# What lies behind, added by sixteen 32 by 32 products instead of four of 32 by 128; the bias of the exponentials as an operand

## The chip, the cores and the metric

The kernel runs on one core of a Trainium2 chip. The metric is the time of an execution on the device in microseconds. An engine of the core is named as in the profile: PE is TensorE (PEld its weight loads), DVE is VectorE, ACT is ScalarE, POOL is GpSimd, SP is SyncE, which issues most DMAs. A name with a q at its end is that engine's sequencer.

## What is computed

The input x has 4096 rows of 64 numbers, adj is a 4096 by 4096 matrix of zeros and ones (64 MB of float32). Each row of x is normalized, clipped at zero and multiplied by a weight matrix; every row of the output is x plus a weighted sum of these rows. The neighbours of a row (the non-zero columns of adj) are ranked from the left, and only the last 100 count: the rightmost one has weight 1, and the weight halves with each step to the left.

```python
h = jnp.maximum(_layernorm(x, axis=-1), 0.0)
support = h @ weight
mask = (adj != 0).astype(support.dtype)
rank = jnp.cumsum(mask, axis=1)
deg = rank[:, -1:]
k = jnp.minimum(deg, 100.0)
pos = rank - (deg - k)
w = mask * jnp.where(pos > 0, 0.5 ** (k - pos), 0.0)
out = x + w @ support + bias
```

## The kernel before

The weight of a neighbour depends on how many neighbours stand to its right. The kernel finds this number with matrix products, writes it so that one byte holds the exponent, and lets an exponential on ACT turn the byte into the weight.

Rows are worked on in groups of 512 (W), and for each group the right half of the columns first, then the left half: 16 units (u) of 512 rows by 2048 columns. A unit has four loads of 1 MB, `load` (L120), issued by SP into eight buffers a_sb; so there are 64 loads in all. SP issues a load when the buffer's last reader, eight loads earlier, is done. For each load:

- `convert` (L341 on DVE, three times L339 on ACT) turns 128 rows of float32 into bytes m.
- `transpose` (L352, PE) turns them, four bytes at a time as one float32, into pt in PSUM; `settle` (L363, L361, DVE) copies this to mt in SBUF. Columns of adj now lie on partitions.

For each unit:

- `totals` (L369, PE) counts the neighbours in stretches of 32 columns: eight products of 128 by 32 weights, two sets of four, the second set added to the first. `split` (L379, ACT) and `divide` (L382, DVE) take the counts apart, `carry` (L388, POOL) brings in what the right half counted.
- `suffix` (L396, PE) adds up what stands to the right of each stretch; `clamp` (L400, DVE) limits it and writes `behind`, [128, 512] in float16.
- `place(u, a)`, twice a unit, a = 0 and 1 (L407 and L412, PE), makes four tiles v, each 128 by 512 float32, one bank of PSUM. Tile j takes what lies behind from the 32 partitions 32j to 32j+31 of `behind`, through the matrix `where` (L407, a product with 32 rows and 128 columns of weights, which begins the sum in the bank), and then, 32 by 32, the count inside each stretch from `tri` (L412, sixteen products, four on each tile, which end it). There are five buffers for v, so a place needs the release of three of the four tiles of the place before it; the last wait is on the fourth product of L407.
- `weigh` (L420, ACT), once for each v, reads two of the four bytes of every word of v, 1024 bytes on each partition, and writes the exponential to wk. Its scale is -ln 2 and its bias -38 ln 2. There are 128 weigh instructions: 122 on whole tiles, and 6 on half tiles for the last three tiles of all. Three of the last tiles are done on DVE and POOL instead (`encode` L426, `take` L431, `lower` L439, then `gather`).
- `aggregate` (L453, PE) multiplies wk with the support rows hr (two parts, high and low) into acc.

For each group of 512 rows `drain` (L469, ACT, with the bias of the layer as a [128,1] operand bias_sb; the very last half L467 on DVE), `turn_back` (L476, PE) and `finish` (L483, L484, DVE) add the sum to x; `store` (L491) and L486 write it out.

What runs when is set by a list of tasks with costs in nanoseconds and due times, from which the order on each engine is planned while the program is built; a table of shifts (L497 to L523) changes the due times by hand. After that each engine runs its instructions strictly in this order. Neither the costs nor the shifts are touched by the change. L193 makes a [128,1] tile `floor` that holds -38 ln 2; the kernel before does not read it.

Of the kernel before, what the change touches and what calls it, by code (L numbers as in the profile page):

```python
# [8 lines left out]
F32 = mybir.dt.float32  # L9
# [6 lines left out]
U8 = mybir.dt.uint8  # L16
AF = mybir.ActivationFunctionType
# [8 lines left out]
SUB = 32  # L26
UNIT = 2.0 ** -9
LN2 = 0.6931471805599453
# [3 lines left out]
def kernel(  # L32
# [34 lines left out]
    nc = tc.nc  # L67
    P = 128
# [9 lines left out]
    W = TG * P  # L78
# [24 lines left out]
    ps_v = ctx.enter_context(tc.tile_pool(name="ps_v", bufs=NV, space=bass.MemoryType.PSUM))  # L103
# [68 lines left out]
    for h in range(H):  # L172
        q = slice(h * D, (h + 1) * D)
# [18 lines left out]
    floor = const.tile([P, 1], F32, name="floor")  # L192
# [3 lines left out]
    where = const.tile([P, 2, P], F16, name="where")  # L196
# [131 lines left out]
    low, codes, masks, words, wts, accs, tots, pts, sums8, behind, vs, signed = {}, {}, {}, {}, {}, {}, {}, {}, {}, {}, {}, (1, 7, 15)  # L328
# [73 lines left out]
    def place(u, a):  # L402

        for j in range(4):
            v = vs[u, 4 * a + j] = ps_v.tile([P, W], F32, tag="v", name="v")
            q = slice(SUB * j, SUB * (j + 1))
            nc.tensor.matmul(v, where[q, a, :], behind[u][q, :], start=True, stop=False, skip_group_check=True)  # L407
        for c in range(4):
            for j in range(4):
                q = slice(SUB * j, SUB * (j + 1))  # L410
                m = masks[u][q, c, :, a] if UNITS[u][2] == CB else masks[u][q, c % 2, :, c // 2]
                nc.tensor.matmul(vs[u, 4 * a + j][SUB * c:SUB * (c + 1), :], tri[q, q], m, start=False, stop=True,  # L412
                                 skip_group_check=True)

    def weigh(u, k, part=None):
        r = slice(0, W) if part is None else slice(part * W // 2, (part + 1) * W // 2)
        if not part:
            wts[u, k] = wpool.tile([P, 2, W], F32R, name="wk")
        v = vs[u, k] if part == 0 else vs.pop((u, k))
        nc.scalar.activation(wts[u, k][:, :, r], v.bitcast(U8).rearrange("p (i f) -> p f i", f=4)[:, :2, r], AF.Exp, scale=-LN2, bias=-38.0 * LN2)  # L420

    def encode(u, k):

# [150 lines left out]
    for u, (g, c0, cb) in enumerate(UNITS):  # L574
# [9 lines left out]
        for k in range(2 * cb):  # L584
            due = at + k
            if k % 4 == 0:
                task(place, (u, k // 4), PE, due, 800, 920, [("clamp", u), ("constants", 1)], ("v", *(("encode" if (u, k + j) in QUICK else "weigh", u, k + j, *((1,) if u == U - 1 and k + j in PARTED else ())) for j in range(4))))
            if u == U - 1 and k in PARTED:
                continue
            weighs = "weigh"  # L590
            piece_of = block(u, k) // (HB // 2)
            if (u, k) in QUICK:
                weighs = "take"
                task(encode, (u, k), DVE, due - 8, 1160, 1300, [("place", u, k // 4), ("convert", NT - 2)])
                task(take, (u, k), DVE, due - 8, 690, 820, [("encode", u, k)], ("w", ("gather", u, k)))
                task(lower, (u, k), POOL, due - 8, 1200, 1300, [("second", piece_of // 2, piece_of % 2), ("convert", NT - 3)])
            else:
                task(weigh, (u, k), ACT, due + 2.5, 1000, 1130, [("place", u, k // 4)], ("w", ("aggregate", u, k)))
            task(gather if (u, k) in QUICK else aggregate, (u, k), PE, due + 14, 480, 720, [(weighs, u, k), ("lower", u, k) if (u, k) in QUICK else None, ("second", piece_of // 2, piece_of % 2)] +
                 ([("drain", g - 1)] if g and head and k == 0 else []))  # L600
        for part in range(2 if u == U - 1 else 0):
            for k in PARTED:
                due = at + k + part
                task(weigh, (u, k, part), ACT, due + 2.5, 570, 700, [("place", u, k // 4)], None if part else ("w", ("aggregate", u, k, 1)))
                task(aggregate, (u, k, part), PE, due + 14, 260, 500, [("weigh", u, k, part)])
# [20 lines left out]
    while kinds:  # L626
        heads = []
        for kind, keys in kinds.items():
            f, args, engine, rank, hold, lag, needs, pool = tasks[keys[0]]
# [10 lines left out]
        f, args, _, _, hold, lag, _, pool = tasks[key]  # L640
# [11 lines left out]
    for at, _, f, args in sorted(order, key=lambda o: o[:2]):  # L652
        if f in (turn, spread, support, count, transpose, totals, suffix, place, aggregate):
            if end is not None and at - end > 700:
                warm(int(at - end) // 215)
            end = None if f is spread or end is None else at + tasks[f.__name__, *args][4]
        f(*args)
# [37 lines left out]
```

## Time and profile before

| | |
|---|---|
| median of 3 runs | 190.86 us (190.5 to 191.04) |
| the profiled execution | 190.5 us, of which the span of the profile is 188.8 us |
| granted PE clock | mean 0.979 of full speed |
| PE busy | 171.8 us (91%), 1499 products |
| PE weight loads busy | 107.7 us (57%) |
| DVE busy | 161.7 us (86%) |
| ACT busy | 149.5 us (79%); L420 120.0 us of it, x128, mean 1015 ns |
| POOL busy | 20.4 us (11%) |
| HBM | 367 GB/s over the span |
| L407 | 128 products of 32 by 128, mean 383 ns |
| L412 | 512 products of 32 by 32, mean 394 ns |

The span is what the profiler saw of the program; 1.7 us of the execution's time lie around it. Busy times of PE overlap: products are pipelined, and the time of one is longer than the distance to the next. A row of the timeline shows when a run of like instructions began, how long it was from its first start to its last end, which engine and line, what it wrote and read, and how many there were; brackets hold the idle time before it and what ended it. A row of a source line shows the shortest, median and longest time of one instruction in nanoseconds, then the first and last start.

### The profile page before, as it was taken

The numbers are of one execution on the slowest core, as the hardware profiler recorded it, in microseconds if no ns is written. First come the engines' busy times: TensorE is split into PE (matmuls) and PEld (weight loads), VectorE is DVE, ScalarE is ACT, GpSimd is POOL, SyncE is SP. The second block draws the span as 40 slices with busy tenths as digits, with TensorE's granted clock in tenths as the row PEclk, the third lists the DMA queues.
The fourth block names the chain that finished last, engine by engine and source line by source line (L and its number), as shares of the span: only waits on it lengthen the run. The fifth ranks groups of instructions, "written<-read, shape, count | busy, mean of one in ns | idle before, by whom it ended". The sixth has DMA issues, their size and how long they took to land.

```text
span 188.8 us, 3797 instructions
## 1 busy us (share of the span) xinstructions
PE 171.8 (91%) x1499; PEld 107.7 (57%) x1499; DVE 161.7 (86%) x221; ACT 149.5 (79%) x176; POOL 20.4 (11%) x60
## 2 busy tenths in 40 slices
PE   7879979898989999999979997999799999999980
PEld 5657746655555565466546554655366545554560
DVE  4834758899999999999999989998999899996743
ACT  2298055789899896999897889787978997899970
POOL 7000035020001000100020002000100029001000
PEclk9999687999999999999999999999999999999998
DMA  6999999999999999999999999999999999931000
GB/s 212 417 422 422 415 427 420 417 415 420 420 422 420 420 417 418 429 422 413 422 420 420 422 417 418 420 425 418 420 422 410 424 420 418 418 128 62 21 3 28
DMA packets 10338, 69.49 MB, mean 368 GB/s; under 512 B 1360, under 2 KB 1616, under 8 KB 2128
## 3 DMA queue, kind: packets, MB, share of 16 engines
q1 hardware_dynamic: 10016, 69.15, 88.6%
q8 instruction: 12, 0.20, 0.4%
q10 hardware_dynamic: 304, 0.10, 0.2%
q14 instruction: 6, 0.05, 0.1%
HBM read 68.19 MB, written 1.05 MB: 367 GB/s over the span
## 4 chain that ended last, share of the span: by engine, by line
PE 49%; DVE 29%; DMA 10%; ACT 5%; POOL 3%; issue 2%; POOLq 0%; ACTq 0%; DVEq 0%
PE acc L453 18%; DVE m L341 13%; DMA a_sb<-in_adj_dram 10%; PE pt L352 10%; DVE mt L363 6%; PE v L412 4%; PE v L407 4%; ACT wk L420 3%; PE pc L265 2%; PE tot L369 2%; PE pd L281 2%; PE ps L396 2%; DVE behind L400 2%; PE po L476 2%; ACT mt L260 1%
## 5 line engine op out<-in xcount | busy, mean ns | idle before, releaser
L420 ACT ACTIVATE wk<-v 128x1024 fp32r<-128x1024 uint8 (+1 forms) x128 | 120.0, 1015 | 15.3 <-PE v L412 14.9
L341 DVE TENSOR_SCALAR m<-a_sb 128x2048 uint8<-128x2048 f32 x61 | 84.9, 1394 | 4.2 <-DMA a_sb<-in_adj_dram 4.1
L453 PE MATMUL acc<-wk,hr 128*128 128x512 f32 (+1 forms) x256 | 77.7, 421 | 1.1 <-ACT acc_sb L469 0.6
L453 PEld LDWEIGHTS acc<-wk,hr 128*128 128x128 f32 x256 | 43.4, 189 | 18.6 <-issue 6.3
L352 PE MATMUL pt<-ident,m 128*128 128x128 f32 x256 | 41.2, 286 | 6.0 <-DVE m L341 5.4
L363 DVE COPY mt<-pt 128x512 uint32<-128x512 uint32 x61 | 41.7, 685 | 4.3 <-PE pt L352 4.3
L352 PEld LDWEIGHTS pt<-ident,m 128*128 128x128 f32 x256 | 29.7, 145 | 20.6 <-PE acc L453 4.8
L388 POOL COPY sums<-behind 1x512 f16<-1x512 f16 x8 | 6.8, 852 | 129.6 <-ACT sums L379 109.5
L407 PE MATMUL v<-behind,where 32*128 32x512 f16 x128 | 13.7, 383 | 1.5 <-DVE behind L400 1.1
L412 PE MATMUL v<-mt,tri 32*32 32x512 f16 x512 | 14.2, 394 | 0.0
L379 ACT ACTIVATE sums<-tot 128x512 f16<-128x512 uint8 x16 | 9.7, 608 | 3.5 <-PE tot L369 3.5
L400 DVE TENSOR_SCALAR behind<-ps,excess 128x512 f16<-128x512 f32 x16 | 11.9, 745 | 0.1
L382 DVE CAST sums<-tot 128x512 f16<-128x512 uint8 x16 | 10.9, 683 | 1.1 <-ACT sums L379 1.1
L369 PE MATMUL tot<-mt,band 128*32 128x512 f16 x128 | 10.2, 393 | 0.3 <-DVE mt L363 0.3
L396 PE MATMUL ps<-sums,later 128*128 128x512 f16 x32 | 10.0, 396 | 0.2 <-DVE sums L382 0.2
L407 PEld LDWEIGHTS <-where 32*128 32x128 f16 x128 | 3.7, 90 | 10.3 <-issue 9.8
L412 PEld LDWEIGHTS <-tri 32*32 32x32 f16 x512 | 4.4, 88 | 8.7 <-issue 8.7
L248 PE MATMUL none<-junk 128*128 128x256 bf16 x44 | 7.9, 362 | 1.1 <-DVE junk L133 1.1
L260 ACT ACTIVATE mt<-px 64x512 f32<-64x512 f32 x8 | 4.2, 585 | 4.9 <-PE px L256 4.8
L339 ACT ACTIVATE m<-a_sb 128x2048 int8<-128x2048 f32 x3 | 7.6, 2547 | 0.0
L248 PEld LDWEIGHTS <-junk 128*128 128x128 bf16 x44 | 5.6, 129 | 3.4 <-DVE junk L133 1.1
L272 ACT ACTIVATE xs<-pc 128x512 f32<-128x512 f32 x4 | 2.3, 610 | 6.0 <-PE pc L265 6.0
(87 smaller groups left out, 100.6 us busy)
## 6 DMA issues: line engine op xcount, KB each, us to landing
a_sb<-in_adj_dram SPq DMA_DIRECT2D x64, 1024.0 KB, 16.5
xr<-in_x_dram SPq DMA_DIRECT2D x2, 512.0 KB, 6.3
out_dram<-xr SPq DMA_DIRECT2D x1, 512.0 KB, 18.4
out_dram<-xr SPq DMA_DIRECT2D x1, 384.0 KB, 2.3
out_dram<-xr ACTq DMA_DIRECT2D x1, 64.0 KB, 1.6
out_dram<-xr SPq DMA_DIRECT2D x1, 64.0 KB, 1.7
w<-in_L_gnn_weight_dram ACTq DMA_DIRECT2D x2, 16.0 KB, 6.0
bias_sb<-in_L_gnn_bias_dram SPq DMA_DIRECT2D x1, 0.2 KB, 14.1
```

Source lines behind the costliest of these rows:

```text
L248: nc.tensor.matmul(none[:, :2 * P], junk[:, :P], junk, start=True, stop=True)
L341: nc.vector.tensor_scalar(m_v, a_v, 0.0, 64.0, op0=ALU.not_equal, op1=ALU.add)
L352: nc.tensor.transpose(pts[n][:, c, :], m32[:, c * P:(c + 1) * P], ident)
L363: nc.vector.tensor_copy(mw, pt)
L369: nc.tensor.matmul(tot[SUB * c:SUB * (c + 1), :], band[:, SUB - 12 - 4 * a:2 * SUB - 12 - 4 * a], masks[u][:, c, :, a], start=(a == 0), st ...
L382: nc.vector.tensor_copy(*bytes_of(u, 1))
L396: nc.tensor.matmul(px, later[cb][:r, f, :], sums[:r, f, :], start=(f == 0), stop=(f == 1))
L400: nc.vector.tensor_scalar(behind[u], pts.pop((u, "s")), excess[UNITS[u][2]], float(MAX_NEIGH), op0=ALU.subtract, op1=ALU.min)
L407: nc.tensor.matmul(v, where[q, a, :], behind[u][q, :], start=True, stop=False, skip_group_check=True)
L412: nc.tensor.matmul(vs[u, 4 * a + j][SUB * c:SUB * (c + 1), :], tri[q, q], m, start=False, stop=True, skip_group_check=True)
L420: nc.scalar.activation(wts[u, k][:, :, r], v.bitcast(U8).rearrange("p (i f) -> p f i", f=4)[:, :2, r], AF.Exp, scale=-LN2, bias=-38.0 * LN2)
L453: nc.tensor.matmul(accs[g][:, r], parts.rearrange("p s d -> p (s d)"), wk[:, s, r], start=(k == s == 0 and c0 + cb * E * P == N), stop=(c0 ...
```

## The change

Two things change. In `place` the four products of L407, each with 32 rows by 128 columns of weights, become sixteen products of 32 by 32, one for each tile j and each quarter c of its partitions; they all come before the products of L412, which are left as they were. In `weigh` the bias is no longer a constant in the instruction: it is read from the tile `floor`, one number on each partition. In the changed kernel the two lines of place are L409 and L414, that of weigh L422, and every later line moves by two.

```diff
@@ def place(u, a) @@
         for j in range(4):
-            v = vs[u, 4 * a + j] = ps_v.tile([P, W], F32, tag="v", name="v")
-            q = slice(SUB * j, SUB * (j + 1))
-            nc.tensor.matmul(v, where[q, a, :], behind[u][q, :], start=True, stop=False, skip_group_check=True)
+            vs[u, 4 * a + j] = ps_v.tile([P, W], F32, tag="v", name="v")
+        for c in range(4):
+            for j in range(4):
+                q, o = slice(SUB * j, SUB * (j + 1)), slice(SUB * c, SUB * (c + 1))
+                nc.tensor.matmul(vs[u, 4 * a + j][o, :], where[q, a, o], behind[u][q, :], start=True, stop=False, skip_group_check=True)
         for c in range(4):
             for j in range(4):
                 q = slice(SUB * j, SUB * (j + 1))
@@ def weigh(u, k, part=None) @@
-        nc.scalar.activation(wts[u, k][:, :, r], v.bitcast(U8).rearrange("p (i f) -> p f i", f=4)[:, :2, r], AF.Exp, scale=-LN2, bias=-38.0 * LN2)
+        nc.scalar.activation(wts[u, k][:, :, r], v.bitcast(U8).rearrange("p (i f) -> p f i", f=4)[:, :2, r], AF.Exp, scale=-LN2, bias=floor)
```

The order of the instructions on every engine is the same as before, apart from the products that take the place of L407. PE gets 384 products and 384 weight loads more.

## The prediction

> **What bounds the kernel now.** I read the page's slices first, to see which resource is never idle.
>
> ```profile
> DMA  6999999999999999999999999999999999931000
> GB/s 212 417 422 422 415 427 420 417 415 420 420 422 420 420 417 418 429 422 413 422 420 420 422 417 418 420 425 418 420 422 410 424 420 418 418 128 62 21 3 28
> q8 instruction: 12, 0.20, 0.4%
> ```
>
> The DMA engines are full from 5 us to about 165 us at some 420 GB/s, and then empty. The rest, over 20 us, is work behind the last block of adj. The third line is PE's code: twelve packets, 0.20 MB over 12 or 16 KB each. Next the chain of work that ended last, from its long wait on:
>
> ```profile
> 143.64 19.25 DMA a_sb<-in_adj_dram
> ...
> 162.91 1.40 DVE m L341
> 164.32 0.56 DVE mt L363
> 164.88 0.60 DVE sums L382
> 165.48 1.32 DVE m L341
> 166.80 0.63 DVE behind L400
> 167.43 0.60 DVE mt L363
> 168.03 1.31 DVE m L341
> ...
> 176.49 2.07 PE acc L453 x8
> 178.56 0.48 PE v L407 x4
> 179.04 0.38 PE v L412 x13
> 179.41 3.37 PE acc L453 x18
> 182.81 0.48 ACT acc_sb L469
> ```
>
> The block loaded at 143.64 lands at 162.91 and its conversion starts at once. From the semaphore marks of the landings I get 165.39 and 167.86 for the last two blocks, with conversions at 165.41 and 167.95. So **the end is the last landing plus a tail of 21 us**, and what the middle saves is lost again in waiting for DMA. The lag of conversion behind landing falls from 3.3 us (block 17) to 0.0 to 0.4 us (blocks 56 and 57): the middle catches up with room to spare. In the tail PE, DVE and ACT take turns. The ACT rows of the timeline show how little idle time it has there:
>
> ```profile
> 163.62 0.60 ACT L379 ACTIVATE sums<-tot 128x512 f16<-128x512 uint8 x1 [0.49 <-PE tot L369]
> 164.41 3.77 ACT L420 ACTIVATE wk<-v 128x1024 fp32r<-128x1024 uint8 x4 [0.20 <-PE v L412]
> 168.40 1.94 ACT L420 ACTIVATE wk<-v 128x1024 fp32r<-128x1024 uint8 x2 [0.21 <-PE v L412]
> 170.60 0.69 ACT L469 ACTIVATE acc_sb<-acc,bias_sb 128x512 f32<-128x512 f32 x1 [0.26 <-PE acc L453]
> ```
>
> Later there are 0.32 us before 176.67, and then nine weighs in a row until 182.6. ACT is busy 14.07 of the 15.10 us from 167.9 to 183.
>
> **Part 1: the bias becomes a [128,1] operand (L420).** The trace has both kinds of activation at 512 columns:
>
> ```profile
> L379 ACT ACTIVATE sums<-tot x16: 597/603/639, 26.9 to 172.1; 128x512 f16<-128x512 uint8 x16
> ```
>
> ```profile
> L469 ACT ACTIVATE acc_sb<-acc,bias_sb x8: 474/694/739, 55.2 to 182.8; 128x512 f32<-128x512 f32 x7, 128x256 f32<-128x256 f32 x1
> ```
>
> Median 603 ns with a constant, 694 ns with bias_sb as operand: 0.09 us more. It is not the type read: L272, also 128x512 f32 and without the operand, has a median of 604. The next activation starts 0.57 us after a L469 and 0.48 us after a L379, so the 0.09 us is not hidden by overlap. 128 weighs x 0.09 = 11.5 us of ACT work. Bounds: 0 (if the gap were due to Identity or to the output) and 0.14 per weigh (739 less 597, the far ends of the two rows); I take 0.09, by the medians. In the middle a unit lasts 9.9 us (four blocks of 2.48) and ACT works about 8.0 of it (eight weighs 0.905 apart, a split of 0.48, half a drain of 0.57); 8.7 still fits.
>
> **Part 2: sixteen 32x32 products.** They add 12 products and 12 weight loads to each of 32 places: 768 instructions on PE. How long does a place take on PE?
>
> ```profile
> 91.50 0.39 PE L407 MATMUL v<-behind,where 32*128 32x512 f16 x4
> 91.83 0.44 PE L412 MATMUL v<-mt,tri 32*32 32x512 f16 x16
> 92.20 0.50 PE L453 MATMUL acc<-wk,hr 128*128 128x512 f32 x1
> ```
>
> L412 starts 0.33 us after L407, and sixteen 32x32 products start within 0.05 us (0.44 less 0.39), 3.3 ns apart. The nearest row for a second set on the same tiles in the same shape is L369, two sets of four:
>
> ```profile
> 93.30 0.63 PE L369 MATMUL tot<-mt,band 128*32 128x512 f16 x8
> ```
>
> It spans 0.63 us where one product takes 0.39 to 0.40: the second set starts 0.23 to 0.24 after the first. So with one shape throughout I expect L412 0.24 us after L407: **0.09 us less for each place**, 2.9 us of PE in all. Bounds: 0.05 us more (the 0.33 stays and the stagger is added) and 0.11 less (0.22 between the sets).
>
> The Trainium skill has a rule against this change: "TensorE: Matmul & The Clock Gate", section "The mechanism" of Part 3 (its list of what overlaps), says that a weight load overlaps running products only when it is for another row group. Twelve of the sixteen share a row group with an earlier one; by that rule they would come in four turns, by my estimate three turns of 0.2 us more for each place, some 20 us in all. L412 in this trace, sixteen within 0.05 us with each row group four times, says otherwise, and I go by it.
>
> No wait is added. The waits for the four v buffers stand on the first four products in both kernels; 28 instead of 16 products queue behind the fourth, 12 x 3.3 ns = 0.04 us. Behind them PE has the aggregates and transposes. The code grows by 768 of 2,998 instructions, so PE fetches about three packets more. Each fetch makes one of the sixteen DMA engines late for good: the sixteenth completion mark of a block falls 1.25 us behind the others after the first fetch (21.3 us), and a second 1.25 us is lost after the ninth (141.5 us), when the same engine is struck again. About 13 instead of 10 fetches before the last landing: if they go round by eights, two strikes on one engine remain the most, and 167.86 stays. I take 0; one strike more or less is 1.25 us.
>
> **The tail step by step** (starts of before; the changed kernel by the two differences).
> - Four weighs from 164.41 are 0.36 longer in all. The next place needs the third of them: its end moves from 167.29 to about 167.48 (place 0.09 earlier, three weighs 0.27 later), and PE comes at 167.48. The idle 0.21 and the 0.09 of the place take it: next weigh at 168.4. Change 0.
> - Two weighs from 168.40: 0.18, within the 0.26 before L469. Change 0.
> - Weigh at 171.19: 0.09. The split (172.09) ends 172.78 instead of 172.69; DVE, its reader, is busy until 172.94. Change 0, with 0.16 to spare.
> - From 172.57 ACT is late: 0.09, then 0.09 for each weigh. The third release for the place at 175.72 comes at 175.82 instead of 175.45. Its fourth product goes from 175.75 to 175.87, and its last L412 is 0.05 late; weighs go on at 176.72 instead of 176.67.
> - The place at 178.49 was already held by ACT (its four products span 0.55 instead of 0.39). The release it waits for is 0.05 + 2 x 0.09 = 0.23 later, the saved 0.09 is partly taken by the 0.04: the half weighs start 0.18 late.
> - Six half weighs: the fifth ends 0.18 + 5 x 0.09 = 0.63 late; its aggregate had 0.15 to spare. L469 at 182.81 and everything after it, the last aggregate too, which waits for L469, is **0.48 us late**.
>
> With some 0.1 us for the places between 148 and 153 us, where PE was held by ACT as well, the sum is +0.55: 190.5 becomes 191.05 for the profiled execution. That was the fastest of the three shown; against their median, 190.86, the forecast is **191.4 us**. Bounds of the terms: without the gain on PE +0.8, with 0.14 for each weigh +1.0; with 0 for the weighs -0.3.
>
> **Rivals.**
> - The idle time of ACT hides the operand and the tail goes by PE: four places x 0.09 earlier at most, so -0.35 to +0.2 us, 190.5 to 191.1. For it: ACT waits for L412 14.9 us in all. Against it: the chain ends in nine weighs without a gap.
> - The end comes earlier, by code: with 13 fetches in another rhythm no DMA engine is struck twice before the last landing, which then comes at 166.6. It decides from the moment when the ninth fetch goes to a fresh engine. -1.25 + 0.55 = -0.7: 190.2 us. Against it: the late marks look like a round of eight.
> - The reverse, a third strike: +1.25 + 0.55, 192.7 us.
> - The middle falls behind DMA: weighs release v later, places stand, transposes and conversions slip. In eight of the 32 places PE has under 0.3 us to spare against the third release. Should a unit take more than 9.9 us from load 17 on, the 3.3 us of lag stay: +1 to +3.3, 191.9 to 194.2.
> - PE isn't fed: its instructions start on average 53 ns apart from 160 to 180 us (374 of them); 45 would be needed. If 53 were the limit, 96 more in 20 us would cost 5 us there: over 195. All bursts ran 3.3 ns apart, so I hold it unlikely.
>
> The case that the change does not do what it says, no saving between the sets, is the +0.8 above.
>
> **Chances.** Tail lengthened by ACT (+0.2 to +1.0) 0.55, the likeliest; hidden 0.15; fewer strikes 0.08; third strike 0.08; middle falls behind 0.11; not fed 0.03. About 0.3% (0.57 us) is what a measurement of this kernel can tell from no change. Of the first case 0.35 lies beyond that and 0.20 within; hidden lies within, fewer strikes faster, the rest slower: slower 0.57, same 0.35, faster 0.08. The range 190.4 to 192.9 leaves out fewer strikes, not fed and the upper half of the middle's case, 0.16.
>
> **What would show it.** Weigh rows of 1120 instead of 1030 ns; the line of tri starting 0.24 us after the line of where; the last landing near 167.9; ACT without idle time from 172 to the end; 15 code packets. It is wrong if the last landing moves by over 1 us, if the gap between the two lines stays at 0.33, or if conversions of the last blocks start late against their landings.

## The result, and the profile after

The changed kernel takes **192.11 us** (median of 4, 191.84 to 192.20) against 190.76 us (median of 4). The ratio is 1.0068, 95% interval 1.0050 to 1.0086: slower, as forecast, by 1.35 us where 0.55 were forecast. The profiled execution took 192.2 us with a span of 190.5 us, 1.71 us longer than that of before. The table says where they come from; landings and conversions are read from the semaphore marks and the instructions of the two traces:

| us | before | after | difference |
|---|---|---|---|
| last block landed | 167.86 | 168.03 | 0.17 |
| its conversion began behind that | 0.09 | 1.13 | 1.04 |
| from there to the end of the span | 20.84 | 21.34 | 0.50 |

The page of after, its row of weighs and its row of PE's code packets:

```profile
L422 ACT ACTIVATE wk<-v,floor 128x1024 fp32r<-128x1024 uint8 (+1 forms) x128 | 130.2, 1117 | 8.1 <-PE v L414 7.5
...
q8 instruction: 15, 0.25, 0.5%
```

A weigh takes 1117 ns on average, 102 more than the 1015 of before. ACT waits for PE only 7.5 us in all, 14.9 before. The PE rows of the timeline around one place:

```profile
91.76 0.44 PE L409 MATMUL v<-behind,where 32*32 32x512 f16 x16
91.99 0.43 PE L414 MATMUL v<-mt,tri 32*32 32x512 f16 x16
```

The second set now starts 0.23 us after the first instead of 0.33, and a place is 0.10 us shorter. So both parts do on their own instructions what was expected. The chain of work that ended last shows where time was lost:

```profile
152.71 0.63 PE pt L352 x4
153.34 0.30 PE tot L369
153.64 1.01 ACT wk L422
154.66 0.04 issue
154.70 0.43 PE v L409 x13
155.13 0.37 PE v L414 x14
155.50 0.65 ACT sums L379
...
181.48 3.02 ACT wk L422 x5
```

From 143 us on weighs stand in the chain at two places: one at 153.64, for which a place of unit 12 waits, and those of the tail. Before, the chain ran over the DMA of one of the last blocks in the first of these stretches, and over PE in the second. The PE rows of the place of unit 12 say how long it stood:

```profile
153.83 0.39 PE L409 MATMUL v<-behind,where 32*32 32x512 f16 x3
154.70 0.43 PE L409 MATMUL v<-behind,where 32*32 32x512 f16 x13 [0.47 <-ACT wk L422]
```

Three products went out, and the fourth came 0.87 us after the first, because it waited for a v buffer; in the kernel before, the fourth product of this place came 0.34 us after the first.

### The profile page after: what moved, and what is told of

Read it like the earlier page. It is cut to its first block, busy times and chain, and to the rows that moved or that the text cites. A ratio compares the mean times of both kernels' runs of the same rounds, so it can differ in the third digit from the quotient of the medians.

```text
span 190.5 us, 4566 instructions
## 1 busy us (share of the span) xinstructions
PE 170.4 (89%) x1883; PEld 106.3 (56%) x1883; DVE 161.6 (85%) x221; ACT 159.6 (84%) x176; POOL 20.5 (11%) x60
## 3 DMA queue, kind: packets, MB, share of 16 engines
HBM read 68.19 MB, written 1.05 MB: 363 GB/s over the span
## 4 chain that ended last, share of the span: by engine, by line
PE 50%; DVE 28%; DMA 10%; ACT 7%; issue 2%; POOL 1%; POOLq 0%; ACTq 0%; DVEq 0%
PE acc L455 17%; DVE m L341 13%; PE pt L352 10%; DMA a_sb<-in_adj_dram 10%; DVE mt L363 5%; PE v L409 5%; ACT wk L422 4%; PE tot L369 3%; PE v L414 3%; PE ps L396 3%; PE pc L265 2%; PE pd L281 2%; DVE sums L382 2%; PE po L478 2%; DVE behind L400 1%
## 5 line engine op out<-in xcount | busy, mean ns | idle before, releaser
L422 ACT ACTIVATE wk<-v,floor 128x1024 fp32r<-128x1024 uint8 (+1 forms) x128 | 130.2, 1117 | 8.1 <-PE v L414 7.5
L455 PE MATMUL acc<-wk,hr 128*128 128x512 f32 (+1 forms) x256 | 79.2, 424 | 1.7 <-ACT wk L422 1.1
L409 PE MATMUL v<-behind,where 32*32 32x512 f16 x512 | 16.1, 384 | 1.7 <-ACT wk L422 0.9
L414 PE MATMUL v<-mt,tri 32*32 32x512 f16 x512 | 15.3, 386 | 0.0
L409 PEld LDWEIGHTS <-where 32*32 32x32 f16 x512 | 5.6, 87 | 12.3 <-issue 11.4
L248 PE MATMUL none<-junk 128*128 128x256 bf16 x44 | 6.7, 324 | 1.1 <-DVE junk L133 1.1
L248 PEld LDWEIGHTS <-junk 128*128 128x128 bf16 x44 | 5.0, 116 | 2.9 <-DVE junk L133 1.1
L471 ACT ACTIVATE acc_sb<-acc,bias_sb 128x512 f32<-128x512 f32 (+1 forms) x8 | 5.4, 670 | 0.8 <-PE acc L455 0.8
```

The source lines that it names most:

```text
L248: nc.tensor.matmul(none[:, :2 * P], junk[:, :P], junk, start=True, stop=True)
L409: nc.tensor.matmul(vs[u, 4 * a + j][o, :], where[q, a, o], behind[u][q, :], start=True, stop=False, skip_group_check=True)
L455: nc.tensor.matmul(accs[g][:, r], parts.rearrange("p s d -> p (s d)"), wk[:, s, r], start=(k == s == 0 and c0 + cb * E * P == N), stop=(c0 ...
```

## The experiments

All are compared with runs of the kernel before on the same chip, 190.76 to 190.85 us.

**One part at a time.** My first theory (A) put a good part of the lost time on the longer code: the ninth code fetch came at 118.6 us instead of 141.5 us, and the block that landed late through it was block 44 instead of 54. The rival (B) gave it all to the operand. The first kernel has the operand alone:

```diff
-        nc.scalar.activation(wts[u, k][:, :, r], v.bitcast(U8).rearrange("p (i f) -> p f i", f=4)[:, :2, r], AF.Exp, scale=-LN2, bias=-38.0 * LN2)
+        nc.scalar.activation(wts[u, k][:, :, r], v.bitcast(U8).rearrange("p (i f) -> p f i", f=4)[:, :2, r], AF.Exp, scale=-LN2, bias=floor)
```

> The kernel before with the bias operand alone; L407 keeps its four products. Theory A (two causes: the operand makes the tail about 0.5 us longer and holds a few places of unit 12; the rest, 0.6 to 0.8 us, comes from the longer code, whose ninth fetch strikes a DMA engine at 118 us instead of 141 us): +0.6 to +1.1 us over the kernel before, the second late mark again near block 54, last conversion 0.2 to 0.5 us late. Theory B (the operand alone makes all of it, by holding the places at 148 to 155 us): +1.3 to +1.7 us, last conversion over 1 us late. Theory C (the sixteen products cost time themselves): +0.5 us at most, the tail alone.

Measured: 192.37 us (6 runs, 191.92 to 193.81), ratio 1.0085 (1.0053 to 1.0116), 1.6 us over the kernel before. Its ninth fetch came at 143.3 us. That is what B said, but the interval reaches down to 1.0 us, so that this run alone does not exclude A. The second has the sixteen products alone, that is the changed kernel with the constant:

```diff
-        nc.scalar.activation(wts[u, k][:, :, r], v.bitcast(U8).rearrange("p (i f) -> p f i", f=4)[:, :2, r], AF.Exp, scale=-LN2, bias=floor)
+        nc.scalar.activation(wts[u, k][:, :, r], v.bitcast(U8).rearrange("p (i f) -> p f i", f=4)[:, :2, r], AF.Exp, scale=-LN2, bias=-38.0 * LN2)
```

> The changed kernel with the constant bias: sixteen products alone. Theory A: the ninth code fetch near 118 us, last conversion 0.5 to 0.8 us late, tail 0.1 to 0.2 us shorter: +0.3 to +0.7 us over the kernel before. Theory B: -0.3 to 0.0 us, since PE saves 0.1 us in each place and ACT is as quick as before. Theory C: +0.5 to +0.9 us, with the last conversion in time and a longer tail.

Measured: 190.52 us (12 runs), ratio 0.9983 (0.9972 to 0.9994): **the products alone are faster**, by 0.24 us. The ninth fetch came at 117.4 us, as in the changed kernel, and yet the last conversion began only 0.29 us after its landing. Theory A falls, and so does C, by which the products cost time themselves. By the medians the parts add up: the operand costs 1.61 us with four products and 1.59 with sixteen; the products save 0.24 us without the operand and 0.26 with it. The two figures that use the run with the operand alone are uncertain by some 0.6 us, by its interval.

**Code by itself.** This was to move the code fetches without touching the steady work: 17 warm-up products were each cut into sixteen small ones.

```diff
     def warm(n):
         for i in range(n):
-            nc.tensor.matmul(none[:, :2 * P], junk[:, :P], junk, start=True, stop=True)
+            if n > 20:
+                nc.tensor.matmul(none[:, :2 * P], junk[:, :P], junk, start=True, stop=True)
+                continue
+            for s in range(4):
+                for c in range(4):
+                    nc.tensor.matmul(none[SUB * c:SUB * (c + 1), 64 * s:64 * (s + 1)], junk[:, SUB * c:SUB * (c + 1)], junk[:, 64 * s:64 * (s + 1)],
+                                     start=True, stop=True)
```

> The kernel before, but 17 of the warm-up products (L248, results unused) are cut into sixteen smaller ones each, in the same time: 510 instructions more for PE, all issued before 18 us, nothing else changed. Theory A: all code fetches after it come two earlier, the ninth near 112 us; last conversion 0.5 to 0.8 us late, tail unchanged: +0.4 to +0.9 us. Theories B and C: no change, within 0.2 us.

> The same longer warm-up code, and the bias operand; four products in L407. Theory A: ninth fetch near 112 us, last conversion 1.0 to 1.5 us late, tail 0.5 us longer and without PE's saving a little more: +1.4 to +2.1 us, at least as slow as the changed kernel. Theory B: the same as the operand alone, +1.3 to +1.7. Theory C: +0.5 us at most.

Measured: 202.89 us, ratio 1.0616 (1.0589 to 1.0642), and with the operand 204.20 us, ratio 1.0692 (1.0667 to 1.0717). No theory had that. The PE rows of the timeline of the first, and from its page the row of PE's granted clock (one digit for each fortieth of the span, in tenths of full speed, 9 for 90% or more):

```profile
15.57 1.43 PE L253 MATMUL none<-junk 128*32 128x64 bf16 x153
21.68 1.79 PE L253 MATMUL none<-junk 128*32 128x64 bf16 x119 [4.67 <-issue]
...
PEclk9999555569999999999999999999999999999999
```

After 153 products with their weight loads, PE stood for 4.67 us with nothing to wait for in the program; a packet with 16 KB of its code arrived in that time. A second such stop, of 2.77 us, came at 25 us. The setup is late from then on, and the granted clock is down to about half from 20 to 44 us, where the kernel before has 9999687 in its first seven slices. The runs do not separate what the stops and what the lower clock each cost of the 12 us. So they show that code this dense makes PE stand, and say nothing about the place of the ninth fetch.

**Where the operand costs.** Theory D: in two stretches in which ACT has no gap, units 11 and 12 and the tail. Theory E: all weighs alike. The bias is chosen by the unit u, with sixteen products in each kernel; of the line of weigh only its end is shown:

```diff
-bias=floor
+bias=floor if u >= 14 else -38.0 * LN2             (e5)
+bias=floor if u < 14 else -38.0 * LN2              (e6)
+bias=floor if u not in (11, 12) else -38.0 * LN2   (e7)
```

> Sixteen products; the operand only for the 16 weighs of units 14 and 15, the constant for the other 112. Against products alone (190.52 us). Theory D (the operand costs in two stretches where ACT has no gap: the tail, and units 11 and 12): the tail's share alone, +0.5 to +0.8, 191.0 to 191.3 us, last conversion in time. Theory E (every weigh counts alike, the middle simply catches up more slowly): 16 of 128, +0.2, 190.7 us.

> Sixteen products; the operand for the 112 weighs of units 0 to 13, the constant in units 14 and 15. Theory D: the share of units 11 and 12 alone, +0.7 to +1.0 over products alone, 191.2 to 191.5 us, last conversion near 169 us, tail from there as short as with products alone (20.5 us of the span). Theory E: 112 of 128, +1.4, 191.9 us.

> Sixteen products; the constant for the 16 weighs of units 11 and 12, the operand for the other 112. Theory D: most of the middle's share is gone: 0.7 to 1.0 under the changed kernel (192.11), 191.1 to 191.4 us; the places of unit 12 are held by 0.25 and 0.34 us again instead of 0.34 and 0.87. Theory E: 0.2 less than the changed kernel, 191.9 us.

| | us | ratio to before (interval) | last conversion behind its landing | from there to the end of the span |
|---|---|---|---|---|
| products alone | 190.52 | 0.9983 (0.9972 to 0.9994) | 0.29 | 20.49 |
| e5, 16 operands | 191.57 | 1.0037 (1.0023 to 1.0050) | 0.37 | 21.35 |
| e6, 112 operands | 191.23 | 1.0025 (1.0015 to 1.0035) | 1.03 | 20.51 |
| e7, 112 operands | 191.48 | 1.0032 (1.0022 to 1.0043) | 0.42 | 21.34 |
| changed kernel, 128 | 192.11 | 1.0068 (1.0050 to 1.0086) | 1.13 | 21.34 |

Sixteen operands in the tail cost 1.05 us, more than 112 before it (0.71 us), and constants in units 11 and 12 alone win back 0.63 us. D is nearer than E in all three, though only e6 lies in its range: the tail is 0.25 us dearer in the median than D's upper bound, and e7 is 0.1 us above it. The two columns at the right separate: with the operand in the tail the last stretch is 0.85 to 0.86 us longer, whatever stands before it; with the operand in units 11 and 12 the last conversion is 0.7 to 0.8 us later. The fourth product of unit 12's second place comes 0.34 us after the first in e7, as with products alone, 0.85 us in e6 and 0.87 us in the changed kernel.

The ACT rows show why it is these units. First the changed kernel:

```profile
142.16 3.13 ACT L422 ACTIVATE wk<-v,floor 128x1024 fp32r<-128x1024 uint8 x3 [1.29 <-PE v L414]
145.17 0.60 ACT L379 ACTIVATE sums<-tot 128x512 f16<-128x512 uint8 x1
145.65 7.42 ACT L422 ACTIVATE wk<-v,floor 128x1024 fp32r<-128x1024 uint8 x7
152.92 0.72 ACT L471 ACTIVATE acc_sb<-acc,bias_sb 128x512 f32<-128x512 f32 x1
```

And products alone:

```profile
145.16 1.06 ACT L422 ACTIVATE wk<-v 128x1024 fp32r<-128x1024 uint8 x1
146.71 5.63 ACT L422 ACTIVATE wk<-v 128x1024 fp32r<-128x1024 uint8 x6 [0.49 <-PE v L414]
```

With the constant ACT still waits 0.49 us at 146.7; with the operand it works without a gap from 142 us on, and every further 0.1 us is handed to the next place. The plan has put the last place of unit 11 and the two of unit 12 close together there. In the kernel before they stand 3.6 and 4.3 us apart, where half a unit has 5.0 us at the pace of the loads, and ACT has one gap of 0.61 us between them:

```profile
145.18 0.39 PE L407 MATMUL v<-behind,where 32*128 32x512 f16 x4
146.09 5.74 ACT L420 ACTIVATE wk<-v 128x1024 fp32r<-128x1024 uint8 x6 [0.61 <-PE v L412]
148.75 0.62 PE L407 MATMUL v<-behind,where 32*128 32x512 f16 x4
153.03 0.71 PE L407 MATMUL v<-behind,where 32*128 32x512 f16 x4
```

The ACT rows of the tail, changed kernel first and then products alone:

```profile
173.87 10.63 ACT L422 ACTIVATE wk<-v,floor 128x1024 fp32r<-128x1024 uint8 x13
```

```profile
172.86 9.71 ACT L422 ACTIVATE wk<-v 128x1024 fp32r<-128x1024 uint8 x13
```

Thirteen weighs without a gap in both; 10.63 instead of 9.71 us.

**The plan.** If the dense stretch of the plan is the cause in the middle, another plan should not have it. The planner allows 1400 ns for a late landing at load 54, where the kernel before has it; with sixteen products it is at load 44.

```diff
-            lag += 1400 if key in (("load", 6), ("load", 54)) else 0
+            lag += 1400 if key in (("load", 6), ("load", 44)) else 0
```

With products alone:

> Sixteen products with the constant, and a plan of its own: the planner's allowance of 1400 ns for a late landing stands at load 44, where the trace of products alone has it, instead of load 54. That moves tasks of units 10 to 13 on all engines. If the plan's dense stretch at 143 to 157 us, made for a late landing at load 54, costs the 0.3 us by which the last conversion is late, 190.2 us; the table of shifts was tuned for the old place, so up to 191.0 us if these matter more.

Measured: 190.35 us (11 runs), ratio 0.9977 (0.9968 to 0.9986), 0.4 us faster than the kernel before and the lowest median of all; its interval overlaps that of products alone. The last conversion begins 0.10 us after its landing. The two places of unit 12 now stand 5.6 us apart, at 148.2 and 153.8 us, and both go out unhindered. With the whole change:

> The changed kernel (sixteen products and the operand in all 128 weighs) with the plan of the run before: allowance for the late landing at load 44. In that plan the two places of unit 12 had 1.5 and 1.4 us to spare with the constant. Theory D, with the middle's share a matter of the dense stretch in the old plan: last conversion within 0.3 us of its landing, only the tail's 0.85 us is left: 191.1 to 191.4 us. If the operand holds the middle in any plan: 0.6 to 0.8 us more, 191.9 to 192.2 us.

Measured: 191.27 us, ratio 1.0023 (1.0013 to 1.0033), clear of the changed kernel's 1.0068. The last conversion is in time (168.05 us), and from there 21.34 us are left, as in every kernel with sixteen products and the operand in the tail. So the operand costs the middle nothing once the dense stretch is gone, and the tail's share stays in both plans: 191.27 less 190.35 is 0.92 us. Last, the kernel before with that plan:

> The kernel before (four products, constant) with the same new plan. Its ninth code fetch is expected near 141 us still, so plan and landing no longer fit: if that fit is what the plan's place is worth, +0.2 to +0.6 us over the kernel before, 191.0 to 191.4 us; if the new plan is simply the better order, -0.2 to 0.0, 190.5 to 190.8 us.

Measured: 190.83 us, ratio 0.9997 (0.9985 to 1.0010), no change, with its ninth fetch at 141.6 us. It neither loses by a plan that does not fit its late landing nor gains by it. That the fit of allowance and landing is what made e8 faster is therefore not shown; what is shown is that with its order the last conversion starts in time.

## Why the prediction was right in sign and short in size

- **The operand, 0.09 us a weigh**: right. 1126 ns instead of 1030 in the median.
- **The places, 0.09 us less**: right, 0.10 (0.23 instead of 0.33 us between the two sets). The rule of the Trainium skill against the change ("TensorE: Matmul & The Clock Gate", "The mechanism" of Part 3) did not hold: the sixteen products of L409, each row group four times, span 0.44 us where one takes 0.39, as L412 did before, and not four turns.
- **Code**: right. Fifteen packets; just after the ninth, as before, the sixteenth mark of a block came late, by 1.4 us and 22.9 us earlier than before. That this is the engine struck first is inferred from these marks, since the profile names no engine for a packet of code. The last landing moved by 0.17 us. Neither rival with a strike more or less came true, nor the one in which PE isn't fed: all sixteen still start within 0.05 us.
- **The tail step by step, 0.48 us**: measured 0.50. Products and operand pull against each other in it, -0.35 and +0.85 us by the table, and the walk along ACT's rows had caught both. It holds in its steps too: the fourth product of the place at 175.72, counted from the last conversion, was forecast 0.12 us later and came 0.12 us later. The bound without the gain on PE, +0.8 us, is also what the operand alone shows there: 21.64 us from the last conversion on, 0.80 more than before.
- **The term that failed is "some 0.1 us for the places between 148 and 153 us, where PE was held by ACT as well"**. It measured 1.04 us: 0.84 by the operand (1.13 less 0.29) and 0.20 with the products alone. I had walked the tail weigh by weigh, but weighed the middle by its mean: 8.7 of 9.9 us of ACT for each unit, and room to catch up. The mean hides that the plan bunches three places into 7.8 us, with only 0.61 us of idle time on ACT between them. By an estimate from the medians, eleven weighs from 142 us to the fourth product at 154.7 are 1.0 us longer; against products alone 0.5 of it uses up the gap, and 0.53 holds the place. The same rows were there to be read in the trace of before. So was another sign: I took the lags of blocks 56 and 57, 0.0 and 0.4 us, for room to spare, but blocks 55 and 58 of that trace are 1.11 and 0.84 us behind.
- Of the rivals, **the middle that falls behind** was the right mechanism, at 0.11. It did so not from load 17 on but in one stretch: at block 53 the changed kernel was only 0.03 us behind its landing, at block 58 it was 1.97 (products alone 1.16). A stretch that late has ten blocks or fewer to make it good, and 1.13 us were left at the end.
- Of the three signs of being wrong that the prediction names, the last came true: the conversions of the last blocks start late against their landings. The measured +1.35 us also lies above the highest bound of the sum's terms, +1.0; it lies within 190.4 to 192.9 us because that range takes in the lower half of the rival.
- Two sums of the prediction are slightly off and decide nothing: 0.48 and some 0.1 us are 0.58 and not 0.55, and 374 and 96 instructions in 20 us need a distance of 43 ns and not 45.
- My theory after the result, that the earlier late landing had cost 0.6 to 0.8 us, was wrong as well: with the products alone the late landing is there, and the last conversion is 0.29 us behind, 0.20 more than before.

## What to carry to other kernels

Two sets of products of one shape followed each other 0.10 us sooner here than two of different shapes, even with four times as many products in the first; each of the sixteen had a 32 by 32 tile of its own, and the added code came in time. A constant that an instruction can carry should not be read from a tile on an engine that has stretches without a gap. Here 0.1 us for each of 128 instructions, 10 us of ACT's busy time in all (130.2 against 120.0), lengthened the kernel by 1.6 us, and that came from two such stretches; so look for them in the engine's own rows and not in its mean share. Where an order is planned ahead, the bunches in the plan can set the price of a slower instruction.

## What the runs showed of the hardware

PE's code comes over the DMA engines that carry the data: the profile of after counts 15 packets of code, 0.25 MB, among their work, about 16 KB each. With the engines full of loads (419 GB/s from 15 to 20 us), 153 products and their weight loads within 1.43 us were followed by a stop of 4.67 us, and that kernel took 12 us more, at a lower granted clock for part of them. The 768 instructions that the change adds, spread over 32 places, caused no such stop: in its trace no product waits without a cause in the program, and no weight load does so for longer than 0.8 us.

The granted clock of PE in the setup differs from execution to execution, and so does how far conversion is behind landing at block 17. The clock rows of the pages of operand alone and products alone:

```profile
PEclk9999558999999999999999999999999999999998
```

```profile
PEclk9999999999999999999999999999999999999997
```

They are behind by 4.67 and 1.65 us; the kernel before (9999687 at the start) by 3.30, the changed one (9999756) by 3.55. The smallest lag goes with the full clock, but the clock alone does not set it: operand alone and changed kernel both spend 10.2 us at half clock in the setup, from 20.0 and from 21.5 us on, and their lags differ by 1.1 us. Products alone, before and changed kernel have worked the lag off to 0.05, 0.54 and 0.03 us by block 53. The operand alone, in this execution of 193.75 us, had not: 2.67 us at block 53 and 2.43 at the end. Its six executions took 191.9 to 192.4 us four times and 193.8 twice. With ACT slower and no gain on PE the middle may catch up too slowly after such a start; one execution has a trace, so this is not shown.
